# Four bias adds moved from the end of layer 0 into layer 1's products, and five pairs of output rows sent as one transfer each

## The chip, the cores and the metric

The kernel runs on one core of a Trainium2 chip. The core has five engines that run on their own instruction queues and meet through semaphores: TensorE (PE in the profile; its weight loads are PEld), VectorE (DVE), ScalarE (ACT), GpSimd (POOL) and SyncE (SP, which here only issues transfers). Sixteen DMA engines move data between the chip's memory and the core. The metric is device microseconds (us) of one execution, and lower is better; a kernel's time is the median of several runs.

## The reference, cut to what matters

A graph of 2,500 nodes with 256 features and 80,000 directed edges, sorted by target, goes through a normalisation, three layers of edge convolution and a final product with all four feature sets side by side. The result is added to the input.

```python
h = jnp.maximum(_layernorm(x, axis=-1), 0.0)
xs = [h]
for W, b in ((W0, b0), (W1, b1), (W2, b2)):
    # _edge_conv: mean over a node's incoming edges of [x_i, x_j - x_i] @ W + b
    h = jax.nn.relu(_edge_conv(h, src, dst, W, b))
    xs.append(h)
return x + jnp.concatenate(xs, axis=-1) @ Wf + bf
```

Two things matter below. The final bias `bf` is one row of 256 numbers that is added once to every node's output. The output itself can be built up piece by piece: the part of `Wf` that belongs to a layer's features can be applied and added as soon as those features exist.

## The kernel before

**The data.** Nodes are kept in 20 tiles of 128 rows (the last has 68), taken as ten pairs. The edges become a 2,560 by 2,502 matrix of counts, in five groups of columns (four of 504 columns, one of 486). It is built group by group, used for layer 0 from the core's own memory, and stored in the chip's memory (`a_dram`) for layers 1 and 2. `acc`, 128 partitions by 20 tiles by 256, holds the output as it is summed up. `hT` holds the current features, transposed. `zh` and `zl` are the two halves (high and low) of the features times a weight, so that two products give nearly fp32.

**The order of work.** Nearly all instructions go through `InOrder`, a helper at line 282 that keeps them in program order on their engine. All of them therefore carry L282 in the profile, and are told apart by the names of their tiles. `general` is a fallback that this input does not enter: at the end, each engine reads a flag `missing` and branches past it. ACT, DVE and PE do so only behind the transfer `near_end`.

**Layer 0's end.** `layer` (line 861) runs group by group, and between its units of PE work the loop at line 1068 draws one step from a chain of other work, `extra`. For the last group that chain ends with `first_forms` (line 1030): it prepares layer 1's weights, splits the first two pairs of `hT` into three parts each (`Split`: one ACT copy, then two DVE operations), and then adds `bf_sb` to `acc` in four instructions, five tiles each. `run(extra)` issues what is left.

**Layers 1 and 2** each have two stages. The first (line 1354, "the node stage" below) goes over the ten pairs. For each pair PE does twelve products of the split parts with the weights; ACT and DVE turn the result into `zh`, `zl` and sums of them (`parts`, `combine`, `sums`), and DVE adds the part for the output to `acc` (`add_to_acc`). A call `split(order[i + 2])` prepares the pair two ahead, again one ACT copy and two DVE operations into a tile named `staged`. Two turns late, PE also multiplies a pair with the fifth group of counts (`lone`).

The second stage (`Stream`, line 1307, "the stream" below) multiplies with the four other groups, taken two at a time, in ten chunks of seven steps. A step is four products on PE with one block, and `make` (line 1319) prepares blocks up to five steps ahead (`LEAD`). The seven blocks of a chunk are `b11`, `b21`, `b22` (ACT casts), `r1` and `r2` (a DVE sum in place, then an ACT cast), and `r3`, `r4` (DVE). The sum for `r2` overwrites `b22`, so it waits for ACT's cast of `b22`. Before the stream begins, only two blocks are ready: `stream.make(2)`.

**The end** (line 1412) goes over the ten pairs in the order 8, 9, 0, 1, 2, 3, 7, 6, 5, 4. PE multiplies each pair's features with the last part of `Wf`, DVE adds the result to `acc`, one instruction for each tile of 128 rows, and after each tile a transfer sends it to `out`. SP issues all of these, apart from the second tile of the last four pairs, which ACT issues.

Of the kernel before, what the change touches and what calls it, by code (L numbers as in the profile page):

```python
# [313 lines left out]
def by_windows(ctx: ExitStack, tc: tile.TileContext, x, src, dst, Ws, bs, Wf, bf, out, missing):  # L314
    nc = tc.nc
    PE, DVE, ACT, POOL, SP = nc.tensor, nc.vector, nc.scalar, nc.gpsimd, nc.sync
    PEo, DVEo, POOLo, ACTo, SPo = (InOrder(tc, e) for e in (PE, DVE, POOL, ACT, SP))
    P = 128
# [29 lines left out]
    Q = NT // 2  # L348
# [23 lines left out]
    def bank():  # L372
        return ps[-1].tile([P, 512], F32, name="bank")


    acc = const.tile([P, NT, D], F32, name="acc")
# [586 lines left out]
    def flat(l):  # L963
        return raws[l].rearrange("p c t d -> p c (t d)") if l < L else wfs[l]
# [61 lines left out]
    def split_in_blocks(q, whole=True):  # L1026
        two = [block().rearrange("p c n -> p (c n)") for _ in range(2)]
        return Split(q, [two[0][:, :2 * D], two[0][:, 2 * D:], two[1][:, :2 * D]], whole)

    def first_forms():  # L1030
        DVEo.tensor_sub(ws[1][0], ws[1][0], ws[1][1])
        yield
        coming.append(Forms(flat(1), [flat(1)[:, c, :] for c in range(DC)]))
        coming[0].high()
        coming[0].low()
        yield
        coming[0].across()
        coming[0].last()
        yield
        for q in range(2):  # L1040
            split_in_blocks(q)
            yield
        for t in range(0, NT, 5):
            DVEo.tensor_add(acc[:, t:t + 5, :], acc[:, t:t + 5, :], bf_sb.unsqueeze(1).to_broadcast([P, 5, D]))
            yield

    extra = chain(degrees(0), finish(0, a), later_loads(), degrees(1))
    for g in range(NG):
        at = {}
        own = [NT] * 4 if g == 0 else [3, 3, 8, 8]  # L1050
        if g + 1 < NG:
            a1 = new_a(g + 1)
            one = build(g + 1, a1)
            left = -(-len([b for b in windows if b[0] == g + 1]) // TURN)
            units = NT + DC * DC
            at = {(i + 1) * (units - 4) // left - 1 for i in range(left)}
            if g:
                own = [sorted(at)[j] + 1 for j in ((5, 6, 9, 10) if g == 1 else (2, 3, 7, 8))]
        else:
            second.close()  # L1060
            raw_pools.append(ctx.enter_context(tc.tile_pool(name="raw", bufs=1, side="right")))
            bf_sb = raw_pools[-1].tile([P, D], F32, name="bf_sb")
            load_wb(1, SPo)
            load_wf(1, SPo)
            SPo.dma_start(bf_sb, bass.AP(tensor=bf.tensor, offset=bf.offset, ap=[[0, P], [1, D]]))
            ready = ctx.enter_context(tc.tile_pool(name="ready", bufs=7, side="right"))
            extra = chain(shares(), (None for _ in range(4)), first_forms())
# [54 lines left out]
    def times(to, split, i, forms):  # L1122
        for c in range(DC):
            for k in range(3):
                PEo.matmul(to, split.parts[k][:, c, i * P:(i + 1) * P], forms.parts[k][:, c, :],
                           start=(c == 0 and k == 0), stop=(c == DC - 1 and k == 2))

    def add_to_acc(t, po):
        DVEo.scalar_tensor_tensor(acc[:, t, :], po, share[:, t:t + 1], acc[:, t, :], op0=OP.mult, op1=OP.add)
# [40 lines left out]
    class Pair:  # L1170
# [12 lines left out]
        def make(self, c, what, st, made):  # L1183
            to = made[what] = block()[:, :, :GS]
            b11, b21, b12, b22 = (st[:, g, h::2, :] for g in range(2) for h in range(2))
            if what[0] == "b":
                ACTo.copy(to, {"b11": b11, "b21": b21, "b22": b22}[what])
            elif what == "r1":
                DVEo.tensor_add(b12, b11, b12)
                ACTo.copy(to, b12)  # L1190
            elif what == "r2":
                DVEo.tensor_add(b22, b12, b22)
                ACTo.copy(to, b22)
            elif what == "r3":
                DVEo.tensor_sub(to, b11, b22)
            else:
                DVEo.tensor_add(to, b22, b21)
# [109 lines left out]
    class Stream:  # L1307
# [11 lines left out]
        def make(self, upto):  # L1319
            while self.n < min(upto, len(self.steps)):  # L1320
                m, p, c, part, what, made = self.steps[self.n]
                p.make(c, what, self.loaded[m], made)
                self.n += 1
                if self.n == len(self.steps) or self.steps[self.n][0] != m:
                    self.load(m + 4)
# [15 lines left out]
    def split(q):  # L1341
        tile_ = stage.tile([P, 4 * GS], F32R, name="staged")
        Split(q, [tile_[:, k * 2 * D:(k + 1) * 2 * D] for k in range(3)])

    begun = []
    for l in range(1, L):
        order = orders[l]
        lone = Alone(l, order)
# [5 lines left out]
        for i in range(Q + LAG):  # L1354
            if 0 < i <= Q:
                lone.make(i - 1)
            if i < Q:
                q = order[i]
                n = Nodes(l, q)
# [53 lines left out]
    for i, q in enumerate(order):  # L1413
        po = bank()
        po = [po[:, :D], bank()[:, :D] if i == Q - 1 else po[:, D:]]
        for k in range(2):
            if q in PLAIN:
                for c in range(DC):
                    PEo.matmul(po[k], hT[:, c, (2 * q + k) * P:(2 * q + k + 1) * P], wfs[L][:, c, :],
                               start=(c == 0), stop=(c == DC - 1))  # L1420
            else:
                times(po[k], splits[q], k, coming[0])
        for k in range(2):
            t = 2 * q + k
            add_to_acc(t, po[k])
            n = P if t < NT - 1 else LAST
            d = (ACTo if i >= Q - 4 and k else SPo).dma_start(out[t * P:t * P + n, :], acc[:n, t, :])
            if i == Q - 2:
                near_end = d
        if i == 0:  # L1430
            begun[0].rest()
        elif i == 1:
            split_in_blocks(3)
        elif i < 4:
            split((5, 4)[i - 2])
# [3 lines left out]
def gnn_kernel(tc: tile.TileContext, x, src, dst, Ws, bs, Wf, bf, out):  # L1439
    nc = tc.nc  # L1440
    with tc.tile_pool(name="flag", bufs=1) as flag:
        missing = flag.tile([1, 1], I32, name="missing")
        tc.mark_branch_hint_location("again", "LikelyTaken",
                                     engines=[getattr(mybir.EngineType, e) for e in ("PE", "DVE", "Activation")])
        near_end = by_windows(tc, x, src, dst, Ws, bs, Wf, bf, out, missing)
        loads, (again,) = nc.values_load_multi_w_load_instructions(missing, min_val=0, max_val=1)

        for d in loads:
            if d.ins.engine in [getattr(mybir.EngineType, e) for e in ("PE", "DVE", "Activation")]:
                tc.add_manual_dep(d.ins, near_end.ins.name,  # L1450
                                  mybir.DependencyInfo(mybir.DependencyClass.Sync, mybir.DependencyReason.DATA),
                                  reason="behind the outputs")
        with tc.If(again > 0, label="again"):
            general(tc, x, src, dst, Ws, bs, Wf, bf, out)
# [28 lines left out]
```

## Time and profile before

| | |
|---|---|
| time, median of 3 runs | 471.52 us (471.42 to 471.71) |
| the profiled execution | 472.05 us, span of its instructions 470.2 us |
| PE busy, matmuls | 462.6 us, 98% of the span |
| DVE, ACT, POOL busy | 380.8, 310.7, 41.4 us |
| adds of `bf_sb` to `acc` | 4, 128x1280, 1.48 us each, at 199.6 to 205.3 us |
| outputs on SP's queue | 15 of 128 KB and one of 68 KB, at 452.5 to 465.3 us |
| outputs on ACT's queue | 4 of 128 KB, at 462.9 to 465.9 us |

The profile lists instructions with their start, their length, and in brackets how long their engine stood idle before them and which event ended that. Consecutive instructions of one engine overlap by some 0.1 us at their ends, so the distance from start to start is the honest cost of one in a row. The time of an execution is some 1.9 us longer than the span: what lies around the first and last instruction.

### The profile page before, as it was taken

How to read it: one execution, taken by the hardware profiler on the slowest of the kernel's cores; microseconds unless marked ns; L12 is line 12 of the kernel's file. 1: busy time of each engine (PE TensorE's matmuls, PEld its weight loads, DVE VectorE, ACT ScalarE, POOL GpSimd, SP SyncE). 2: the span in 40 equal slices, each digit the busy share in tenths (PEclk: the TensorE clock that was granted, in tenths of full speed). 3: DMA queues.
4: the chain of work that ended last, by engine and by line, in shares of the span. 5: the costliest groups of instructions: out<-in, count | busy, mean ns of one | idle time of the engine just before them, and what ended most of it. 6: DMA issues, size and time to landing. Idle time of an engine off the chain costs nothing.

```text
span 470.2 us, 7370 instructions
## 1 busy us (share of the span) xinstructions
PE 462.6 (98%) x2739; PEld 365.7 (78%) x2739; DVE 380.8 (81%) x699; ACT 310.7 (66%) x543; POOL 41.4 (9%) x66
## 2 busy tenths in 40 slices
PE   8999999999999999999999999999999999999995
PEld 4888888787778878877887877877788788688685
DVE  8989898799898873499987847877899687578795
ACT  5777677685754441478769857785787798397540
POOL 3691015200101001000000000000000000000000
PEclk9999999999999999999999999999999999999998
DMA  8320084990824608531178551010212955220014
GB/s 277 93 55 3 1 165 78 193 215 13 178 44 84 139 0 166 113 118 59 46 237 313 177 176 55 36 45 1 88 44 89 352 177 199 88 89 0 1 62 160
DMA packets 21791, 52.07 MB, mean 111 GB/s; under 512 B 1959, under 2 KB 12150, under 8 KB 21750
## 3 DMA queue, kind: packets, MB, share of 16 engines
q1 hardware_dynamic: 14390, 33.41, 21.3%
q0 software_dynamic: 5856, 16.51, 18.3%
q10 hardware_dynamic: 1504, 1.63, 1.0%
q8 instruction: 22, 0.36, 0.3%
q14 instruction: 19, 0.16, 0.1%
HBM read 36.08 MB, written 15.46 MB: 110 GB/s over the span
## 4 chain that ended last, share of the span: by engine, by line
PE 89%; DVE 8%; DMA 1%; ACT 0%; issue 0%; DVEq 0%
PE bank L282 85%; PE pz L282 4%; DVE acc L282 2%; DVE st L282 1%; DVE one_m L282 1%; DMA acc<-in_x_dram 1%; DVE zl L282 1%; DVE one_n L282 1%; DVE staged L282 1%; DVE tmp L282 0%; DVE mv L282 0%; PE turned L282 0%; DVE kn L282 0%; DVE rs L282 0%; ACT junk L282 0%
## 5 line engine op out<-in xcount | busy, mean ns | idle before, releaser
L282 ACT CAST block<-staged 128x1008 fp32r<-128x1008 bf16 x120 | 117.9, 1031 | 16.7 <-DVE staged L282 6.4
L282 PE MATMUL bank<-block,zh 128*128 128x504 f32 (+1 forms) x200 | 83.7, 419 | 0.0
L282 PE MATMUL bank<-a,zh 128*128 128x504 f32 (+1 forms) x200 | 81.7, 408 | 0.0
L282 ACT CAST a<-bank 128x480 fp32r<-128x480 f32 (+1 forms) x105 | 54.4, 561 | 38.0 <-PE bank L282 36.2
L282 PE MATMUL bank<-a,zl 128*128 128x504 f32 (+1 forms) x200 | 77.8, 389 | 0.0
L282 PE MATMUL bank<-block,zl 128*128 128x504 f32 (+1 forms) x200 | 77.3, 387 | 0.0
L282 DVE TENSOR_TENSOR one_m<-iota_m,key_m 128x2048 bf16<-128x2048 bf16 (+2 forms) x55 | 64.4, 1171 | 9.9 <-PE bank L282 9.7
L282 PE MATMUL bank<-block,sh 128*128 128x504 f32 x160 | 68.9, 431 | 0.0
L282 PE MATMUL bank<-block,staged 128*128 128x512 f32 (+1 forms) x288 | 63.5, 370 | 0.3 <-DVE staged L282 0.2
L282 PE MATMUL bank<-block,sl 128*128 128x504 f32 x160 | 62.6, 391 | 0.0
L282 PEld LDWEIGHTS bank<-block,staged 128*128 128x128 f32 x288 | 49.2, 188 | 11.3 <-DVE staged L282 1.6
L282 DVE TENSOR_TENSOR block<-staged 128x1008 fp32r<-128x1008 bf16 x40 | 47.0, 1205 | 5.4 <-PE bank L282 4.1
L282 DVE TENSOR_TENSOR one_n<-iota_n,key_n 128x960 bf16<-128x960 bf16 (+2 forms) x110 | 51.3, 507 | 0.0
L282 PEld LDWEIGHTS <-one_m 128*128 128x128 bf16 x834 | 37.3, 97 | 13.9 <-issue 7.7
L282 PEld LDWEIGHTS bank<-block,zh 128*128 128x128 f32 x200 | 37.6, 188 | 10.8 <-issue 2.5
L282 PEld LDWEIGHTS bank<-block,zl 128*128 128x128 f32 x200 | 37.6, 188 | 10.6 <-issue 3.5
L282 PE MATMUL bank<-one_n,one_m 128*128 128x120 bf16 x834 | 44.7, 204 | 0.2
L282 PEld LDWEIGHTS bank<-a,zh 128*128 128x128 f32 x200 | 37.8, 189 | 6.4 <-issue 0.2
L282 PEld LDWEIGHTS bank<-a,zl 128*128 128x128 f32 x200 | 37.7, 189 | 6.3 <-issue 0.2
L282 DVE TENSOR_TENSOR staged<-staged 128x1008 bf16<-128x1008 bf16 x40 | 27.2, 679 | 17.4 <-ACT block L282 17.0
L282 PE MATMUL pz<-wbf,hT 128*128 128x256 f32 x160 | 38.8, 387 | 0.3 <-ACT hT L282 0.2
L282 PEld LDWEIGHTS bank<-block,sh 128*128 128x128 f32 x160 | 30.1, 188 | 10.4 <-issue 3.5
(163 smaller groups left out, 616.4 us busy)
## 6 DMA issues: line engine op xcount, KB each, us to landing
staged<-a_dram SPq DMA_DIRECT2D x52, 504.0 KB, 4.4
a_dram<-a POOLq DMA_DIRECT2D x20, 630.0 KB, 10.3
acc<-in_x_dram POOLq DMA_DIRECT2D x3, 640.0 KB, 11.9
out_dram<-acc SPq DMA_DIRECT2D x15, 128.0 KB, 1.7
acc<-in_x_dram SPq DMA_DIRECT2D x2, 512.0 KB, 8.9
wbf<-in_L_gnn_Wf_dram SPq DMA_DIRECT2D x4, 256.0 KB, 8.9
acc<-in_x_dram ACTq DMA_DIRECT2D x1, 768.0 KB
wbf<-in_L_gnn_W_dram SPq DMA_DIRECT2D x3, 256.0 KB, 6.1
```

What stands on the lines that cost most here:

```text
L282: return self.tc.keep_in_program_order(call(*args, **kwargs))
```

## The change

The four adds of the bias leave `first_forms` and become a generator `add_bf` of their own. `make` draws one step from it ahead of every block `r2`. The generator yields twice for each add, so the adds come ahead of `r2` in chunks 0, 2, 4 and 6 of layer 1's stream; layer 2's stream finds it empty. At the end, the pairs 8, 0, 1, 2 and 3 go out as one transfer of 256 rows each, issued by SP after the pair's second add. Pair 9 (whose last tile has 68 rows) and the last four pairs are sent as before.

```diff
         for q in range(2):
             split_in_blocks(q)
             yield
+
+    def add_bf():
         for t in range(0, NT, 5):
             DVEo.tensor_add(acc[:, t:t + 5, :], acc[:, t:t + 5, :], bf_sb.unsqueeze(1).to_broadcast([P, 5, D]))
+            yield
             yield
@@ Stream.make
                 m, p, c, part, what, made = self.steps[self.n]
+                if what == "r2":
+                    next(bias, None)
                 p.make(c, what, self.loaded[m], made)
@@
-    begun = []
+    begun, bias = [], add_bf()
@@ the last loop
             add_to_acc(t, po[k])
             n = P if t < NT - 1 else LAST
-            d = (ACTo if i >= Q - 4 and k else SPo).dma_start(out[t * P:t * P + n, :], acc[:n, t, :])
+            if i < Q - 4 and q < Q - 1:
+                if k:
+                    d = SPo.dma_start(out[(t - 1) * P:(t + 1) * P, :].rearrange("(k p) d -> p k d", p=P),
+                                      acc[:, t - 1:t + 1, :])
+            else:
+                d = (ACTo if i >= Q - 4 and k else SPo).dma_start(out[t * P:t * P + n, :], acc[:n, t, :])
             if i == Q - 2:
                 near_end = d
```

## The prediction

> **What bounds the kernel now.** I read the page's busy times and its chain first, then the chain in order of time, then the weight loads (PEld) and DVE rows at the places it points to.
>
> ```profile
> PE 462.6 (98%) x2739; PEld 365.7 (78%) x2739; DVE 380.8 (81%) x699; ACT 310.7 (66%) x543; POOL 41.4 (9%) x66
> ...
> PE 89%; DVE 8%; DMA 1%; ACT 0%; issue 0%; DVEq 0%
> ```
>
> PE sets the time nearly everywhere, at full granted clock (PEclk reads 9 in all slices but the last), so an edit on another engine is worth only what it changes in PE's waits. The chain in order of time (start, length, what) names the one place after layer 0's start where DVE holds PE:
>
> ```profile
> 199.89 5.37 DVE acc L282 x4
> 205.26 0.61 DVE staged L282
> 205.90 0.69 DVE staged L282
> ...
> 212.72 252.64 PE bank L282 x1094
> 465.38 0.48 DVE acc L282
> ```
>
> The four bias adds stand between layer 0's last matmul and the split of pair 2 (`staged`), which PE needs for its third pair. After 212.72 the chain is PE up to the last output. PE's waits there, in the weight loads:
>
> ```profile
> 205.56 0.19 PEld L282 LDWEIGHTS bank<-block,staged 128*128 128x128 f32 x1 [0.22 <-issue]
> 205.97 0.19 PEld L282 LDWEIGHTS bank<-block,staged 128*128 128x128 f32 x1 [0.22 <-DVE staged L282]
> 206.64 2.16 PEld L282 LDWEIGHTS bank<-block,staged 128*128 128x128 f32 x10 [0.49 <-DVE staged L282]
> ...
> 211.99 0.19 PEld L282 LDWEIGHTS bank<-block,staged 128*128 128x128 f32 x1 [0.37 <-DVE staged L282]
> 212.72 2.16 PEld L282 LDWEIGHTS bank<-block,staged 128*128 128x128 f32 x10 [0.54 <-DVE staged L282]
> ...
> 216.70 2.73 PEld L282 LDWEIGHTS bank<-block,staged 128*128 128x128 f32 x12
> ```
>
> PE waits for pair 2 and again for pair 3, and from pair 4 on no more. The brackets sum to 1.62 us, but that is not the loss: a weight load stands idle while the product before it runs. The loss is read against layer 2, which runs the same products with no adds in front:
>
> ```profile
> 331.46 0.19 PEld L282 LDWEIGHTS bank<-block,staged 128*128 128x128 f32 x1 [0.22 <-issue]
> ...
> 341.58 2.73 PEld L282 LDWEIGHTS bank<-block,staged 128*128 128x128 f32 x12
> ```
>
> From the third pair's first load to the fifth pair's first load it is 341.58 - 331.46 = 10.12 us in layer 2 and 216.70 - 205.56 = 11.14 us in layer 1. The adds cost PE 1.02 us, not the 5.6 us that DVE spends on them.
>
> **The change part by part.**
>
> *Adds taken from the node stage: -1.02 us.* An add costs DVE (205.18 - 199.57) / 4 = 1.40 us from start to start. Without them pair 2's split waits only for ACT's copy (200.41, 0.62 us long), and its two DVE operations (0.72 + 0.61 us) end by 202.5; PE asks at 205.97. What is late next? DVE then follows PE: pair 1's `zl` cannot start before ACT's `zh` ends at 206.48; `zl` 0.60, two output adds 0.78, `combine` 0.99 bring it to 208.9, pair 3's split ends at 209.6 (low) and 210.3 (across). PE wants them at 205.56 + (337.03 - 331.46) = 211.1 and later: over 1 us to spare. From there a turn takes DVE 1.33 (split) + 0.60 (`sl`) + 0.60 + 0.78 + 0.99 = 4.30 us and PE 341.58 - 337.03 = 4.55 us, so the margin grows. I count the whole 1.02. No transfer moves with the adds, so SP's and POOL's queues stay as they are. Bounds: 1.02 at the most, about half if pair 3's split still comes late.
>
> *Adds put into the stream: 0.* Each stands between the sums for `r1` and `r2`, where DVE idles until ACT has cast `b22`:
>
> ```profile
> 251.14 0.69 DVE L282 TENSOR_TENSOR staged<-staged 128x1008 bf16<-128x1008 bf16 x1 [2.75 <-ACT block L282]
> ...
> 260.76 0.68 DVE L282 TENSOR_TENSOR staged<-staged 128x1008 bf16<-128x1008 bf16 x1 [1.10 <-ACT block L282]
> ```
>
> For chunks 0, 2, 4 and 6 this idle time is 2.75, 1.10, 1.88 and 1.17 us. An add of 1.40 fits twice, and overruns by 0.30 (chunk 2) and 0.23 (chunk 6). Behind the overrun on DVE stand the sum for `r2`, then `r3` and `r4`; ACT waits for `r2`, PE for all three. Two covers: blocks are made five steps ahead, a step is four loads of 0.23 = 0.91 us, so PE uses them 4.6 us later; and DVE's next idle time (0.27 before chunk 3's `r3`, 1.17 in chunk 7) takes the delay up. Chunk 0 has no such lead: PE waits there at 251.16, 252.09 and 253.03, 0.15 us each, for ACT's casts as they come. But these gaps stand in layer 2 too (376.05, 376.98, 377.92), and the add, starting at 248.3 behind `r1`, ends at 249.8, 1.3 us before `b22`'s cast lets `r2` start. Bounds: 0, or 0.53 us if PE paid both overruns.
>
> [...]
>
> *Five merged transfers: 0 on the way.* SP issues a row transfer in 0.33 to 0.41 us and then waits for DVE; the queue's own wait before pair 2's output is typical:
>
> ```profile
> SPq L282 <- DVE acc L282: 1.2, 1, 1.2
> ```
>
> Nothing waits for an early output. [...] The merged ones hold back their first half by the 0.42 us between two issues (460.91 and 461.33). Only pairs 2 and 3 come near the end. The DMA engines are busy at 0.8 to 1.0 from 462 to 466.5 us, but pair 5's and 4's first outputs already land 1.31 us after issue as in the quiet stretch (464.48 to 465.79, 465.27 to 466.58), so a backlog of 0.4 us at 462 is gone by then. Bounds: -0.1 to +0.4 us at the last landing.
>
> *The end: -0.20 us.* After the last output SP passes one wait after another, 0.066 us each: the last landing lets it go at 468.27, and the span ends at 470.2. The outputs use eight semaphores in turn, and SP waits for the eight in a fixed order. Now the last output counts on the fifth, and three waits stand behind it (468.35, 468.41, 468.48). With five transfers fewer, the program of the changed kernel puts the last output on the eighth, and those three are passed before it lands: 3 x 0.066 = 0.20.
>
> *A part I leave at zero:* in the last output (issued 465.90), 15 DMA engines end at 467.26, one at 467.79, since it was fetching instructions from 466.73 to 467.40. That fetch comes as ACT, DVE and PE pass `near_end` (466.68). Both ends move alike, so I expect the same collision; without it the end is 0.5 us earlier.
>
> **Sum.** The profiled execution takes 472.05 us: -1.02 - 0.20 gives 470.83. It lies 0.53 above the median of the runs shown, and I carry the difference over: 471.52 - 1.22 = 470.30 us. About 0.2% (0.94 us) is what a measurement of this kernel can tell from no change; 470.58 is that bound.
>
> **The rivals.**
>
> *Part of the stall stays, or the end gives it back.* For it: ACT must have pair 3's copy and pair 1's `zh` done in time, and it has four other things to do there; the merged transfers could push the last landing by up to 0.4. Against it: over 1 us of margin on DVE and the quiet latencies of the last outputs. Half the stall: 471.52 - 0.51 - 0.20 = 470.81. Whole gain and a last landing 0.4 late: 470.70. No change, by the bound.
>
> *The collision at the end goes.* If `near_end` lands 0.4 us later than before against the last output, the fetch comes after that engine's eight packets: 470.30 - 0.5 = 469.80. For it: pairs 2 and 3 shift DMA work by 0.4 us. Against: by 464.5 the backlog is gone.
>
> *Slower: the adds land on the stream's path.* One mechanism: DVE reaches `r2` late in the stream, ACT casts it late, PE's product waits. All four exposed cost 4 x 1.40 = 5.61: 471.52 - 1.22 + 5.61 = 475.9. It decides when exposed adds exceed 1.22 + 0.94 = 2.2 us, so two must lie wholly on the path. For it: chunk 0 has no lead. Against: 1.3 us spare at chunk 0 and 4.6 us of lead at the others.
>
> *The change doesn't do what it says:* excluded. On DVE the only moves are the four adds, now ahead of `r2` of chunks 0, 2, 4, 6; PE, ACT and POOL keep their order.
>
> **How the numbers follow.** Forecast as worked (470.0 to 470.58): 0.71. Part lost, 470.58 to 471.5: 0.17, most of it under 470.9. Collision gone, 469.6 to 470.0: 0.07. Slower: 0.05. Faster is 0.71 + 0.07 = 0.78. The range 469.6 to 470.9 holds the first and third case and most of the second.
>
> **What would show it.** In the profile after: no wait of PE for `staged` between 204 and 217, and 10.1 us from the third to the fifth pair's first load; four adds at about 247, 258, 269 and 291 us, with `r2` of chunk 0 one microsecond earlier than now and `r2` of chunks 2 and 6 some 0.2 to 0.3 less early; no new wait in the weight loads up to 330; the last landing and SP's passing of it 1.0 earlier, the span's end 1.2 earlier. I am wrong if new brackets on PEld name DVE or ACT in the stream, if the wait at 212 stays, or if the last output lands later after its issue than 1.9 us.

## The result, and the profile after

The changed kernel takes 470.49 us (470.26 to 470.76, median of nine runs) against 471.87 us (471.42 to 472.06, nine runs) for the kernel before, run beside it: a ratio of 0.9973 (95% interval 0.9964 to 0.9982), or 1.38 us less by the medians. The forecast was 470.30 us, in a range of 469.6 to 470.9. It started from 471.52 us for the kernel before, 0.35 less than that kernel took here.

Two lines of the page, busy times and the chain by engine:

```profile
PE 460.8 (98%) x2739; PEld 365.6 (78%) x2739; DVE 380.5 (81%) x699; ACT 311.1 (66%) x543; POOL 41.6 (9%) x66
...
PE 92%; DVE 5%; DMA 1%; ACT 0%; issue 0%
```

DVE has the same 699 instructions and the same busy time to 0.3 us; what went is its share of the chain, 8% to 5%. The chain in order of time ends thus (start, length, what):

```profile
59.73 404.42 PE bank L282 x2330
464.18 0.48 DVE acc L282
```

The four adds and the split behind them, which cut the chain at 199.89, are gone. From 59.73 us on PE alone sets the time, up to the last output's add.

**The node stage.** The weight loads with `staged` (start, length, shapes, idle time before and what ended it):

```profile
205.38 0.19 PEld L282 LDWEIGHTS bank<-block,staged 128*128 128x128 f32 x1 [0.22 <-issue]
205.78 2.51 PEld L282 LDWEIGHTS bank<-block,staged 128*128 128x128 f32 x11 [0.22 <-DVE tmp L282]
210.93 2.75 PEld L282 LDWEIGHTS bank<-block,staged 128*128 128x128 f32 x12
215.49 2.73 PEld L282 LDWEIGHTS bank<-block,staged 128*128 128x128 f32 x12
```

No load waits for `staged` any more. From the third pair's first load to the fifth pair's it is 215.49 - 205.38 = 10.11 us (10.12 unrounded) in place of 11.14, exactly layer 2's stretch. On DVE, pair 3's split now ends long before PE asks for it:

```profile
208.71 0.68 DVE L282 TENSOR_TENSOR staged<-hT,staged 128x512 fp32r<-128x512 f32 x1
209.42 0.69 DVE L282 SCALAR_TENSOR_TENSOR staged<-staged 128x512 fp32r<-128x512 f32 x1
```

It ends at 210.1; the load that needs it stands at 210.93 and after.

**The stream.** The adds and the sums for `r2` in chunks 0 and 2:

```profile
247.09 1.49 DVE L282 TENSOR_TENSOR acc<-acc,bf_sb 128x1280 f32<-128x1280 f32 x1
249.93 0.69 DVE L282 TENSOR_TENSOR staged<-staged 128x1008 bf16<-128x1008 bf16 x1 [1.35 <-ACT block L282]
...
258.36 1.49 DVE L282 TENSOR_TENSOR acc<-acc,bf_sb 128x1280 f32<-128x1280 f32 x1
259.76 0.68 DVE L282 TENSOR_TENSOR staged<-staged 128x1008 bf16<-128x1008 bf16 x1
```

In chunk 0 the add takes 1.40 us of the 2.75 that were idle and leaves 1.35. In chunk 2 `r2` follows the add with no idle time before it, so it comes late, as worked out. What PE shows at chunk 0 is what it showed before, and in layer 2 (the first of three such waits; the other two stand at 250.89 and 251.82):

```profile
249.95 0.19 PEld L282 LDWEIGHTS bank<-block,sh 128*128 128x128 f32 x1 [0.18 <-ACT block L282]
```

From the fifth pair's first load to the last output's add it is 248.68 us, against 248.69 before. The stream pays nothing.

**Where the profiled times differ.** 472.05 - 470.42 = 1.63 us, and the spans differ by 1.68. Layer 1 begins 0.19 earlier (199.27 after 199.46; over all executions profiled for this study this start lies between 198.96 and 199.93 us, whatever the kernel, so this is no part of the change). The node stage gives 1.02. The last output lands 1.75 us after its issue in place of 1.89 (0.14), and SP passes that landing 0.37 us later in place of 0.48 (0.11); both vary that much from one execution to the next. From SP's pass to the end it is 1.70 us in place of 1.90 (0.20). The sum is 1.66.

### The profile page after: what moved, and what is told of

The parts are those of the page before. It is cut to its first block, busy times and chain, and to the rows that moved or that the text cites. A ratio compares the mean times of both kernels' runs of the same rounds, so it can differ in the third digit from the quotient of the medians.

```text
span 468.5 us, 7360 instructions
## 1 busy us (share of the span) xinstructions
PE 460.8 (98%) x2739; PEld 365.6 (78%) x2739; DVE 380.5 (81%) x699; ACT 311.1 (66%) x543; POOL 41.6 (9%) x66
## 3 DMA queue, kind: packets, MB, share of 16 engines
q10 hardware_dynamic: 1504, 1.63, 1.0%
## 4 chain that ended last, share of the span: by engine, by line
PE 92%; DVE 5%; DMA 1%; ACT 0%; issue 0%
PE bank L282 88%; PE pz L282 4%; DVE st L282 1%; DVE one_m L282 1%; DMA acc<-in_x_dram 1%; DVE one_n L282 1%; DVE zl L282 1%; DVE mv L282 0%; PE turned L282 0%; DVE kn L282 0%; DVE rs L282 0%; ACT junk L282 0%; DVE lo_i L282 0%; DVE pick L282 0%; DVE off L282 0%
## 5 line engine op out<-in xcount | busy, mean ns | idle before, releaser
L282 PEld LDWEIGHTS bank<-block,sl 128*128 128x128 f32 x160 | 30.1, 188 | 9.5 <-issue 3.7
```

Of the source, the lines that this page charges most:

```text
L282: return self.tc.keep_in_program_order(call(*args, **kwargs))
```

## The experiments

Each time is a median, with the ratio to the kernel before run beside it (471.98 to 472.22 us). "Node stage" is the stretch of 10.12 us above, "rest" the one of 248.68, "tail" the time from SP's pass of the last landing to the end of the span.

### The change as a whole, and its two halves

The first run is the changed kernel again, beside its halves.

> The changed kernel again, beside the three kernels that take it apart. Expected 1.2 to 1.4 us under the kernel before, as first measured (471.87 to 470.49).

Measured: 470.66 us, 0.9969 (0.9958 to 0.998); node stage 10.12, tail 1.70.

The second has the adds moved and the outputs as they were:

```diff
-            if i < Q - 4 and q < Q - 1:
-                if k:
-                    d = SPo.dma_start(out[(t - 1) * P:(t + 1) * P, :]...)
-            else:
-                d = (ACTo if i >= Q - 4 and k else SPo).dma_start(...)
+            d = (ACTo if i >= Q - 4 and k else SPo).dma_start(...)
```

> The adds moved as in the change, the outputs sent one by one as before. My theory: the adds give the 1.02 us of PE's wait for pairs 2 and 3 and nothing else, and the last output counts on the fifth of the eight semaphores as before, so 1.0 us under before and 0.2 to 0.35 us over the full change. Rival (the adds are the whole gain, the transfers are hidden): as fast as the full change, 1.38 under before. Second rival (the adds cost something in the stream, the transfers give it back): less than 0.8 under before.

Measured: 471.17 us, 0.9977 (0.9968 to 0.9986); node stage 10.12, rest 248.69, tail 1.90. That is 0.81 us under the kernel before and 0.51 over the full change, where 1.0 and 0.20 to 0.35 were expected. The stages are as expected; in this profile layer 1 begins 0.83 us later than in that of the run above.

The third has the merged outputs and the adds at the old place (the same edit of the outputs on the kernel before).

> The five merged transfers alone, the adds at the old place. My theory: 0.20 us under before, all of it behind the last landing (three waits of SP fewer, 0.066 us each); the wait of PE for pairs 2 and 3 stays, 11.1 us from the third to the fifth pair's first load. Rival (hidden transfers): 0. Second rival (five fixed costs of a transfer saved on the way): over 1 us.

Measured: 472.01 us, 1.0001 (0.9992 to 1.0009). The stall is there as before:

```profile
206.88 2.16 PEld L282 LDWEIGHTS bank<-block,staged 128*128 128x128 f32 x10 [0.47 <-DVE staged L282]
...
212.95 2.16 PEld L282 LDWEIGHTS bank<-block,staged 128*128 128x128 f32 x10 [0.54 <-DVE staged L282]
```

Node stage 11.11, tail 1.70. So, by the stages of the traces, the 1.02 us belong to the adds and the 0.20 us of the tail to the transfers. The gain of the transfers shows in the trace and not in the time: the interval leaves -0.4 to +0.4 us, and the last landing in this profile came 1.98 us after its issue. By the times alone the halves do not add up: 0.81 and -0.03 us, against 1.32 for the whole. Each of these differences is uncertain by some 0.4 to 0.5 us, so this does not contradict the split, and does not confirm it.

### Four merged transfers in place of five

```diff
-            if i < Q - 4 and q < Q - 1:
+            if i < Q - 5 and q < Q - 1:
```

One more transfer turns the last output from the last of the eight semaphores to the first, so that SP has all the other waits still before it when it lands.

> The full change with four merged pairs rather than five (pair 3 goes out as two transfers again), so one transfer more at the end. It puts the last output on the first of the eight semaphores, with seven of SP's waits behind it instead of none. Theory (the order of the waits is the gain): 7 x 0.067 = 0.47 us over the full change, although one transfer alone has come back. Rival (each merged pair gives a share of the gain): 0.04 us over it, not to be seen. The span from SP's first pass of the last output to the end should be 0.47 longer.

Measured: 471.38 us, 0.9989 (0.9981 to 0.9998), 0.72 over the full change of the same group; node stage 10.12, tail 2.24. The tail grew by 0.54 us where 0.47 was worked out. SP's waits at the end (waiting instruction, what it waited for, us, times, longest) show a single long one:

```profile
SPq L1463 <- SPq L1463: 2.7, 1, 2.7
```

The full change has four that sum to 2.0:

```profile
SPq L1463 <- SPq L1463: 2.0, 4, 1.0
```

What merging does at the end is thus no saving of transfers: it is the place in the turn at which the last output falls.

### No adds at all

`next(bias)` is left out of `make`, so the bias is missing from the output.

```diff
-                if what == "r2":
-                    next(bias, None)
```

> The changed kernel without the four bias adds anywhere (the bias is left out of the output). It measures what the adds cost at their new place. My theory: nothing; PE's time from the third pair's first load in layer 1 to the last output add is 248.7 us with and without them, within 0.05, and the time is that of the full change. Rival (the overruns of 0.30 and 0.23 us in chunks 2 and 6 reach PE): 0.5 us faster than the full change.

Measured: 473.14 us, 1.0026 (1.0017 to 1.0036): slower than the kernel before, with 5.6 us less work on DVE. Up to the last output nothing differs from the full change: node stage 10.12, rest 248.68. This answers the question it was made for: the adds cost the stream nothing. The loss is all in the tail, 3.71 in place of 1.70 us. SP's waits:

```profile
SPq L1485 <- DVEq L1461: 2.0, 1, 2.0
```

SP waits 2.0 us for DVE's last semaphore. DVE takes its branch past `general` at 466.80, and its next instruction comes at 469.88, 3.1 us later; in the full change it is 0.6 us (466.21 and 466.82). One fetch of instructions is missing here and another is added: in every other run one begins some 10 to 13 us before the last output lands (at 455.8 in the full change, 456.9 in the kernel before), in this run none begins between 444.3 and 465.7, and there is one more at 470.47.

### The adds kept, but short

This run asks whether it is the number of DVE's instructions that decides, or the work in them. The bias reaches four tiles of twenty.

```diff
-            DVEo.tensor_add(acc[:, t:t + 5, :], acc[:, t:t + 5, :], bf_sb.unsqueeze(1).to_broadcast([P, 5, D]))
+            DVEo.tensor_add(acc[:, t:t + 1, :], acc[:, t:t + 1, :], bf_sb.unsqueeze(1).to_broadcast([P, 1, D]))
```

> The full change with each of the four adds cut from five tiles to one (128x256 elements in place of 128x1280; the bias then reaches four tiles of twenty). VectorE keeps the number of its instructions, but each add is short. If the 2.0 us at the end of the kernel without adds came from VectorE's shorter program (where its last block lies, and so what it has to fetch), the tail from SP's pass of the last output to the end is back at 1.70 us, no wait for VectorE shows there, and the time is that of the full change, 470.2 to 471.0 us, since the adds' length is hidden. Rival: what costs the 2.0 us is that VectorE does less work in the stream; then the time is about 472.5 to 473.

Measured: 470.88 us, 0.9973 (0.9963 to 0.9982); node stage 10.12, rest 248.69, tail 1.70, and no wait for DVE in it. With the four instructions back, whatever their length, the 2.0 us are gone. So it is the number of DVE's instructions that decides here, and not the work in them. What ties that number to the missing fetch and to the 3.1 us behind the branch was not shown.

### All four adds ahead of one `r2`

In the next two the adds stand together, ahead of `r2` of chunk 0, which has no lead, and of chunk 2, for which the prediction worked out 4.6 us.

```diff
-                if what == "r2":
-                    next(bias, None)
+                if what == "r2" and c == 0:
+                    run(bias)
```

> All four adds ahead of the block r2 of chunk 0, where blocks have no lead. My theory: the adds run from 247.1 to 252.7 us, the sum for r2 starts at 252.7 instead of 249.9, ACT casts it 2.7 us later, and PE waits 2.7 us before its products with r2: 2.7 us over the full change, 1.4 over the kernel before. Rival (the lead covers it): as the full change. Rival (DVE's time is all on the path): 4.2 us over the full change, since three adds are new there.

Measured: 474.99 us, 1.0056 (1.0041 to 1.007); node stage 10.12, rest 252.89, 4.21 longer. The size is the rival's, three adds at 1.40. The trace shows that the reason is not:

```profile
254.78 0.29 PEld L282 LDWEIGHTS bank<-block,sh 128*128 128x128 f32 x1 [2.85 <-ACT block L282]
254.95 0.33 PEld L282 LDWEIGHTS bank<-block,sl 128*128 128x128 f32 x1
255.38 0.33 PEld L282 LDWEIGHTS bank<-block,sh 128*128 128x128 f32 x1
```

The wait is 2.85 where 0.18 stood (251.82 in the full change), 2.67 more, as the theory had it. But behind it a weight load takes 0.33 us in place of 0.19, and they follow at 0.42 in place of 0.23. The windows (length, busy time of PE, PEld, DVE, ACT and POOL, then the granted clock, the DMA engines' busy share and GB/s):

```profile
252.00:254.80 2.80, 0.38 (x3) 0.01 (x1) 2.70 (x3) 1.10 (x2) 0.00 (x0) 0.98 0.21 86
254.80:258.00 3.20, 3.20 (x8) 2.57 (x9) 3.03 (x7) 2.94 (x4) 0.00 (x0) 0.50 0.27 39
258.00:261.00 3.00, 3.00 (x15) 2.46 (x14) 2.90 (x4) 2.45 (x3) 0.00 (x0) 0.98 0.75 302
```

PE stood still for 2.80 - 0.38 = 2.42 us, and then worked at half clock. Half of some 3.4 us is 1.7, and 2.42 + 1.7 = 4.1 of the 4.21.

With `c == 2` in place of `c == 0`:

> All four adds ahead of r2 of chunk 2, where blocks are made five steps ahead. DVE's idle time there is 1.1 us, so the sum for r2 starts some 4.2 us later than in the full change. My theory: the lead covers most of it; the block is cast by 265.7 where PE asks at about 264.5, so 0.5 to 1.5 us over the full change. Rival (no lead to speak of): 4.2 us over it. Rival (the lead covers all): 0.

Measured: 472.26 us, 1.0011 (1.0002 to 1.002); node stage 10.12, rest 249.86, 1.18 longer, in the range of the theory. On DVE the sum for `r2` follows the adds:

```profile
264.16 0.68 DVE L282 TENSOR_TENSOR staged<-staged 128x1008 bf16<-128x1008 bf16 x1
```

It stood at 259.76 in the full change, and layer 1 begins 0.19 us later here, so it is 4.21 us late, and PE loses 1.18 of that. The lead thus hid 3.0 us and not 4.6: the sum (0.68 us) and ACT's cast of it (1.03 on average) have to fit into the 4.6 as well. The wait that is left:

```profile
266.01 0.19 PEld L282 LDWEIGHTS bank<-block,sh 128*128 128x128 f32 x1 [1.33 <-ACT block L282]
```

PE stands still for 0.9 us here (0.41 busy of 1.30 from 264.70 to 266.00), and the clock stays at 1.00.

### Eight adds at the old place

The kernel before, with each add made twice, so that the bias is in the output twice.

```diff
-            DVEo.tensor_add(acc[:, t:t + 5, :], ...)
+            for _ in range(2):
+                DVEo.tensor_add(acc[:, t:t + 5, :], ...)
```

> The kernel before with eight adds in place of four at the old place in the node stage (the bias is added twice). Theory: of the four adds' 5.6 us VectorE hid 4.6 in its slack there and 1.0 stopped TensorE; the slack is used up, so four more adds cost their whole 5.6 us: the stretch from the third pair's first load to the fifth's is 16 to 17 us in place of 11.1, and the time about 477.6 us. Rival: TensorE pays a fixed share of each add, 1.0 of 5.6: a stretch of 12.2 us and a time of 473.1.

Measured: 479.75 us, 1.016 (1.0143 to 1.0176), 7.53 over the kernel before; node stage 18.97. Both expected numbers were too low. The share is not fixed: the four adds more (5.6 us) cost their whole time here, and then more than that, 7.83 us of the node stage (18.97 - 11.14), for the reason just seen:

```profile
206.50:211.30 4.80, 0.00 (x0) 0.00 (x0) 4.73 (x4) 0.62 (x2) 0.00 (x0) 1.00 0.00 0
211.30:212.10 0.80, 0.00 (x0) 0.00 (x0) 0.79 (x2) 0.00 (x0) 0.00 (x0) 0.51 0.00 0
212.10:218.10 6.00, 5.96 (x12) 4.10 (x13) 5.84 (x14) 2.45 (x5) 0.00 (x0) 0.50 0.08 9
```

PE idles for 5.6 us, and the 6.0 us after that run at half clock, which costs 3.0. Together 8.6 of the 18.97 - 10.12 = 8.85 us lost to the adds.

### The fetch beside the last output

In the kernel before and after, one DMA engine ends the last output 0.4 to 0.5 us behind the other fifteen, beside a fetch of instructions: the fetch ends at 467.40 in the kernel before, and eight rows of the output follow it one by one, from 467.40 to 467.79. That these are one engine's share is an estimate from their number: 128 rows over 16 engines are eight for each. Three runs tried to part the two. The first releases the end blocks of ACT, DVE and PE (each reads the flag and branches past `general`) one pair earlier:

```diff
-            if i == Q - 2:
+            if i == Q - 3:
                 near_end = d
```

> The full change, with near_end taken one pair earlier (pair 6 instead of pair 5), so ACT, DVE and PE read the flag and branch after an earlier output. It tests the collision that I left at zero: an instruction fetch of 0.6 to 0.7 us on one DMA engine holds that engine's share of the last output. Theory (the fetch follows near_end): it starts some 0.8 us earlier, before the last output's packets, which then all land together 0.85 us after the issue plus 0.5: last landing 0.4 us earlier after its issue, 0.4 us under the full change. Rival (the fetch comes with another event, or another fetch takes its place): last landing as it was, no difference.

Measured: 471.10 us, 0.9979 (0.9971 to 0.9988), no gain on the full change (0.9973). DVE and PE pass at 465.13, but ACT still has the last output to issue and passes at 465.57; a fetch of 0.45 us begins at 466.20, among that output's packets, and one DMA engine ends at 467.03, the others at 466.55. The rival held: the fetch did not come earlier, but 1.01 us after the last output's issue, where it is 0.80 in the full change.

The second takes ACT's outputs from it as well, and releases one pair earlier still:

```diff
-                d = (ACTo if i >= Q - 4 and k else SPo).dma_start(...)
-            if i == Q - 2:
+                d = SPo.dma_start(...)
+            if i == Q - 4:
                 near_end = d
```

> The full change, with all outputs issued by SP (none by ScalarE), and the end blocks of TensorE, VectorE and ScalarE released by the output of the fourth pair from the end in place of the second. ScalarE then has nothing left to issue and can read its flag a microsecond earlier, so the fetch of instructions that lay beside the last output's packets should be over before the first of them (about 465.5). Theory: the DMA engine that ends 0.4 to 0.6 us after the other fifteen no longer does, the landing comes 1.3 to 1.4 us after the issue in place of 1.75, and the time is 470.1 to 470.3. Rival: another engine's fetch (VectorE or TensorE, which come later) falls on the same packets, or the end waits are passed in another order: 470.5 to 471.

Measured: 472.75 us, 1.0008 (0.9999 to 1.0017): the whole gain is lost. Node stage, rest and tail are those of the full change, but the last landing comes 3.53 us after its issue:

```profile
SPq L1463 <- SPq L1463: 3.1, 2, 2.6
```

Fifteen DMA engines had ended at 466.7. The sixteenth, with nine packets of each of the last two outputs left, ends at 468.77: four fetches (466.18 to 466.96, 466.67 to 467.09, 466.75 to 467.27, 467.03 to 468.10) stand between its packets. In the full change all but the first of these fetches begin after the landing. With the end blocks released early, the four begin while the outputs are still on their way.

The last run keeps the outputs on SP and puts the release back.

> The full change with all outputs issued by SP, but the end blocks of the other engines released by the second pair from the end, as in the full change: the one half of the run before that moved the outputs, without the half that moved the release. Theory: the 2 us lost there came from the early release, since the engines' end fetches (at 466.2 to 468.1) then met the last two outputs' packets; with the release back in its place those fetches come behind the landing, the last landing is 1.7 to 2.2 us after its issue, and the time is 470.5 to 471.1 us. Rival: it came from the outputs sharing one queue; then the last landing is again about 3.5 us after its issue, and the time is about 472.5.

Measured: 470.57 us, 0.997 (0.996 to 0.998). The wait is gone:

```profile
SPq L1463 <- SPq L1463: 0.8, 2, 0.5
```

So the 2 us came from the early release. Here the first fetch begins at 466.72, behind the landing at 466.65, which comes 1.44 us after the issue: the collision is avoided. What starts that first fetch stays open. In the full change it begins 0.04 us after ACT passes `near_end`; here it is 0.67 us, and 0.63 in the first of these three runs. From SP's last issue it is 1.43, 1.51 and 1.64 us. SP issues one output after another, so the last leaves 0.67 us after its add's start in place of 0.52. From the last add's start to the landing it is 2.11 us, in the two profiles of the full change 2.27 and 2.38. A gain of 0.16 to 0.27 us is in the trace; the times (0.9970 and 0.9973, with intervals of 0.001 each way) don't resolve it. No version tried is shown to beat the changed kernel.

## Why the prediction was right

- **The adds out of the node stage, -1.02.** As worked out, to 0.01 us, in every run without adds there (10.12) and in none with them (11.14 and 11.11, and 18.97 with eight). Reading the loss from start to start against layer 2, and not from the brackets (1.62), gave the right size. What was late next was named rightly too: nothing.
- **The adds into the stream, 0.** Shown by the rest of 248.68 us with the adds, without them, and with short ones. The sums for `r2` came where they were expected: 1.21 us earlier in chunk 0, and 1.00 and 1.06 in chunks 2 and 6, where the overrun takes 0.2. The 0.53 us that the prediction gave as its bound did not come. The cover was smaller than worked out, though: 3.0 us in chunk 2, not 4.6, still well over the overrun of 0.2. The rival that puts all four adds on the path, at 5.61 us, came about in no run. All four in one place without lead cost 4.21 us, and some 1.7 of these were the clock's, for which the rival had no term.
- **Merged transfers, 0 on the way.** Seen as 0. The second rival of the run with the outputs alone, over 1 us for five transfers saved, did not come about: 472.01 us against 471.98. One reading was a little off: by their last packets the first outputs of pairs 5 and 4 landed 1.38 us after issue, not 1.31 (465.86 and 466.65). Pair 2's first output, in the quiet stretch, took 1.36 (460.91 to 462.27), so the conclusion that the backlog was gone stands.
- **The end, -0.20.** Seen in the tail of both kernels with five merged transfers and the old or new adds, and, with the sign turned, as +0.54 with four. By time alone it isn't resolved.
- **The collision, left as it was.** Right for the full change in each of its two profiles. The reason given, that the fetch comes as ACT, DVE and PE pass `near_end`, is not borne out: with `near_end` moved, or the outputs on SP, the fetch did not follow it. In the kernels before and after the two only fall together. That the collision goes was one of the rivals; it came about only with the outputs on SP.
- **What was not in the sum.** The medians differ by 1.38, the sum says 1.22. The remaining 0.16 lies within what the last landing (1.74 to 1.98 us after issue in the runs with ACT's outputs) and the start of layer 1 change from execution to execution. The level, 0.19 us over the forecast, is the sum of two things that partly cancel: the kernel before took 0.35 us more here than in the runs that the forecast started from, and the gain was 0.16 larger. The sign I had set for being wrong, a landing more than 1.9 us after its issue, was too tight: four runs of the experiments lie over it, at 1.91 to 1.98, and the steps tested in them held.

## What to carry to other kernels

Work that nobody waits for is best put where its engine idles and its neighbour has a lead longer than what the work overruns; compare idle time and lead with one instruction, in the trace, place by place. A stop of TensorE should be priced from start to start against a stretch of the same work without it, and the stop of 2.4 us with four adds in chunk 0 as more than its length: it cost 4.21 us, since the granted clock fell to 0.50 behind it. At the very end of a program, look at which semaphore the last transfer counts on, at what the engines fetch then, and at the number of instructions: each of these moved the end in the trace by 0.2 to 2 us with next to no change in the work; the smallest, 0.2, was not resolved in the times.

## What was not expected of the hardware

- **The clock after a stop.** In the stop of 2.4 us, with four adds in chunk 0, the granted clock fell to 0.50; in the one of 0.9 us, with four adds in chunk 2, it stayed at 1.00. The edges can be read from narrow windows. With four adds in chunk 0:

```profile
254.60:254.80 0.20, 0.01 (x1) 0.01 (x1) 0.20 (x1) 0.20 (x2) 0.00 (x0) 0.78 0.00 0
...
258.00:258.20 0.20, 0.20 (x2) 0.20 (x1) 0.20 (x1) 0.20 (x1) 0.00 (x0) 0.69 0.80 242
```

 A mean of 0.78 over 0.2 us puts the fall at 254.71, and 0.69 puts the rise at 258.12: 3.41 us. With eight adds the same reading (0.77 from 211.20 to 211.40, 0.66 from 218.00 to 218.20) gives 211.31 and 218.14: 6.83 us, twice as long, PE being idle for the first 0.8 of it. With four adds the fall came 2.3 us into the stop (from 252.37), with eight 4.8 us (from 206.47). It differs as much at the end of the program: in the kernel before, the last matmul ends at 465.35 and the clock falls 2.1 us later, at 467.48 (a mean of 0.70 from 467.40 to 467.60); in the changed kernel it ends at 464.14, and the clock still reads 1.00 at the span's end, 4.36 us later. What sets the moment was not shown.
- **DVE's branch at the end**: with four instructions fewer on DVE it took 2.5 us longer (3.1 in place of 0.6).
- **The order of SP's last waits**: 0.066 us for each that still lies ahead when the last output lands, 0.20 us for three and 0.54 for seven.
- **Fetches of instructions beside the outputs**: the last eight rows were 0.4 to 0.5 us late beside one fetch, and the last packets 2.1 us late beside four.
